# A message-passing layer on one core: 8-bit bins and places, nine message buffers for six, and two sets of loads issued at other times

## The chip, the core and the metric

The kernel runs on one core of one Trainium2 chip. Its time is the device time of one launch in microseconds; of several launches the median is given. The five engines are named as in the profile: PE multiplies matrices (PEld is its weight load), DVE and ACT work on vectors, POOL is GpSimd, and SP does nothing here but issue DMAs in the order in which they stand in the program. ACT and POOL issue DMAs too.

## The reference, cut to what matters

12500 nodes with 128 features each, 400000 edges sorted by destination, 20 attributes for each edge. The code calls the sorted side `dst` and the random side `src`; messages are *gathered* at `dst` and *summed* at `src`.

```python
h = max(layernorm(x), 0) @ W_in2f.T                      # 12500 x 128
Wij = smu(f_ij @ W_f1.T + b_f1) @ W_f2.T + b_f2          # 400000 x 128, from the 20 attributes
x_ij = h[dst] * Wij * edge_weight[:, None]               # one message for each edge
agg = segment_sum(x_ij, src)                             # 12500 x 128
out = x + smu(agg @ W_o1.T + b_o1) @ W_o2.T + b_o2
```

## The kernel before, in words

**Tiles, groups, supers.** 128 edges are a tile, 4 tiles a group (`GRP`), 2 groups a super (`SUP` = 8 tiles). There are 3125 tiles, 782 groups and 391 supers. The main loop runs over the groups in the order `seq`; its counter is `p`, and the group at `p` is `g`.

**What a group costs.** PE makes the hidden layer (`hide`), ACT bends it (`bend`), PE weighs it (`weigh`, tile `pw`) and gathers the node rows with a one-hot matrix (`gather`, tile `ph`), ACT copies them (`take`, tile `hg`), DVE multiplies the two into the message tile `ms` (`mix`, L997, or L986 and L987 for a paired group). A row of `ms` is 128 features and, as a 129th number, the edge's place within its bin of 128 source nodes.

**Sorting through DRAM.** The sum over `src` is a sort into 98 bins. `bins` and `count` find for each edge the next free row of its bin (DVE marks the bins and keeps running counts, PE counts in tile `pc`, DVE reads it out in L774 and writes row numbers `ix` in L796). POOL then scatters each tile of `ms` to those rows of a DRAM store `buf` with an indirect DMA (`scatter_rows`, L1067): four scatters a group. To have fewer, every third group is paired: two of its tiles are merged into the other two rows' slots (`permute`, `take_pairs`), it takes two scatters, and what did not fit goes out as tile `lt` with a later group, its host, which has five. There are 2933 scatters in all. POOL's scatters stand in no order written by hand, but they follow the groups; PE, DVE, ACT and SP run in the order of the program text.

**Buffers that tie the engines to POOL.** `ms` has six buffers, `ix` eight, `lt` three. An engine that writes one of them waits until the scatter that read it last has landed.

**Epochs and passes.** The supers are cut into ten epochs (`PARTS`). While epoch k is scattered into one store, the store of epoch k-1 is summed in a *pass*: SP fetches chunks of it (`fetch`, L1098, tile `rw`, four buffers), DVE turns the places into a one-hot matrix (`choose`, L1112, tile `se`), PE multiplies (`add`, L1125) and the sums go to `agg`. For epochs 1 to 7 a pass starts with group 7 of the epoch (`LANDED`, called `i` in `chores`): `begin` fetches four chunks, `choose` makes the first one-hot matrix in group 8 and `add` starts in group 9, where it also asks for the second matrix. Each finished chunk fetches the one four ahead. The last two epochs' groups are computed early among the others; their messages are kept in DRAM (`kept_rows`, written by a DMA that ACT issues, L1037) and come back at the end, where only scatters and the last passes are left.

**Chunks of the edge list.** `dst` and `src` come in seven chunks of 512 tiles (`head_of`). For each, `fetched` loads both (SP, L405 and L406, 256 KB each), `based` reads the first destination of each group (DVE, L409), `binned` computes the bins of 128 (`hi_f`, 16-bit float) and `placed` the places (`lo_b`, bfloat16). A timetable of `due` entries says in which slot each stage runs; there are three slots a group. `known`, slot 106, is where the rows of x have all been read.

Of the kernel before, what the change touches and what calls it, by code (L numbers as in the profile page):

```python
# [20 lines left out]
P = 128  # L21
# [8 lines left out]
SUP = 8  # L30
# [20 lines left out]
def gnn_kernel(  # L51
# [294 lines left out]
    with tc.tile_pool(name="ld", bufs=4) as ld, \  # L346
            tc.tile_pool(name="edge", bufs=2) as edge, \
            tc.tile_pool(name="cnt", bufs=3) as cnt, \
            tc.tile_pool(name="msg", bufs=6) as msg, \
            tc.tile_pool(name="row", bufs=4) as rowp, \  # L350
            tc.tile_pool(name="ps1", bufs=1, space=PSUM) as ps1, \
            tc.manual_schedule(engines={ET.PE, ET.DVE, ET.Activation, ET.SP}):
# [36 lines left out]
        def head_of(c, bank=bank):  # L389


            a, n = c * CH, min(CH, NT - c * CH)
            s0, m = a // GRP, (n + GRP - 1) // GRP
            rw = rowp.tile([P, ROWS, ROW], F32, name="rw").rearrange("p q r -> p (q r)")
            di, si, rel = rw[:, 0:n].bitcast(I32), rw[:, CH:CH + n].bitcast(I32), rw[:, 2 * CH:2 * CH + n]
            sf = rw[:, 0:n]
            spare_rows = parts_tile().rearrange("p n k d -> p (n k d)")
            rb = spare_rows.bitcast(U8)[:, :GRP * P].rearrange("p (n e) -> p n e", e=P)
            z = 0 if c else FEW
            base_f = spare_rows.bitcast(F32)[0:1, P:P + CH // GRP]  # L400
            cells = [(j * P, min(P, n - j * P)) for j in range((n + P - 1) // P)]
            kept = [None]

            def fetched():
                nc.sync.dma_start(di, dst_col[:, a:a + n])  # L405
                nc.sync.dma_start(si, src_col[:, a:a + n])  # L406

            def based():
                nc.vector.tensor_copy(base_i[:, s0:s0 + m], di[0:1, 0:n:GRP])  # L409
                nc.vector.tensor_copy(base_f[:, :m], base_i[:, s0:s0 + m])  # L410
                if c == 0:
                    nc.vector.memset(base_f[:, :FEW // GRP], 0.0)
                nc.vector.tensor_copy(rel, di)

            def spread():
                pb = kept[0] = bank("pb")
                flat = pb.rearrange("p j e -> p (j e)")[:, :m * GRP].rearrange("p (s t) -> p s t", t=GRP)
                nc.tensor.matmul(flat, onesb[0:1], base_f[:, :m].unsqueeze(2).to_broadcast([1, m, GRP]),
                                 start=True, stop=True)

            def lowered():
                nc.vector.tensor_sub(rel, rel, kept[0].rearrange("p j e -> p (j e)")[:, :n])

            def turned():
                pd = kept[0] = bank("pd")
                for j, (o, w) in enumerate(cells):
                    nc.tensor.transpose(pd[:w, j, :], rel[:, o:o + w], ident)

            def written():
                w = cells[-1][1]  # L430
                whole = len(cells) - (w < P)
                if whole:
                    nc.scalar.activation(rb[:, :whole], kept[0][:, :whole], AF.Copy)
                    nc.sync.dma_start(rel_dram[0, a * P:(a + whole * P) * P].rearrange("(c t e) -> t c e", t=P, e=P),
                                      rb[:, :whole])
                if w < P:
                    nc.scalar.activation(rb[:w, whole], kept[0][:w, whole], AF.Copy)
                    nc.sync.dma_start(rel_dram[0, (a + whole * P) * P:(a + n) * P].rearrange("(t e) -> t e", e=P),
                                      rb[:w, whole])

            def limits():
                nc.vector.tensor_reduce(lh[:, 0, c:c + 1], rel, op=ALU.min, axis=AX.X)
                nc.vector.tensor_reduce(lh[:, 1, c:c + 1], rel, op=ALU.max, axis=AX.X)

            def bounded():
                most = edge.tile([1, 1], F32, name="most")
                nc.vector.tensor_reduce(most, base_f[:, :early], op=ALU.max, axis=AX.X)
                nc.vector.tensor_scalar(bad[0:1, 2:3], most, float(HEAD * P - WIN), None, op0=ALU.is_gt)
                nc.vector.tensor_scalar(base_i[:, :early], base_f[:, :early], float(HEAD * P - WIN), None, op0=ALU.min)

            def binned():
                whole_bins(hi_f[:, a + z:a + n], sf[:, z:], si[:, z:])

            def placed():
                nc.vector.scalar_tensor_tensor(lo_b[:, a + z:a + n], hi_f[:, a + z:a + n], -float(P), sf[:, z:],
                                               op0=ALU.mult, op1=ALU.add)
# [190 lines left out]
        def mark_bins(s):  # L647
# [8 lines left out]
            m = n // 2  # L656
            nc.vector.tensor_tensor(es[:, :m], eo[:, 0:2 * m:2], eo[:, 1:2 * m:2], op=ALU.add)
            marked[s] = (eo, es)

        def places_of_counts(g, n):  # L660

# [5 lines left out]
        def bins(g):  # L667
# [7 lines left out]
            if g in first:  # L675
                k = first[g]
                m = FEW if g == 0 else tiles_of(k)
                if s_of(g) < EARLY:
                    begins[k] = (t, cnt.tile([P, max(n for _, n in eps_of) * SUP], F32, name="hic", bufs=2))
                else:  # L680
                    begins[k] = (t, cnt.tile([P, eps_of[k][1] * SUP], F32, name=f"hic{k}", bufs=1))
                nc.vector.tensor_scalar(begins[k][1][:, :m], hi_f[:, t:t + m], float(CAP[k]), -BIG, op0=ALU.mult, op1=ALU.add)
# [94 lines left out]
        def number(g):  # L777
# [338 lines left out]
        def add(k, b, q):  # L1116
# [11 lines left out]
                return  # L1128
            if i == SPAN[k] - 1 or b == NB - 1:
                rows_in.pop(c), sel.pop(c)  # L1130
                fetch(k, behind(k, c, AHEAD))
            if g == GRP - 1 or b == NB - 1:
                dst = agg[:, (b - g) * P:(b + 1) * P]
# [54 lines left out]
        LEFT = 24  # L1188

        def few_places():  # L1190
            nc.vector.scalar_tensor_tensor(lo_b[:, 0:FEW], hi_f[:, 0:FEW], -float(P), ssf, op0=ALU.mult, op1=ALU.add)

        def other_starts():
            m = tiles_of(0)
            nc.vector.tensor_scalar(begins[0][1][:, FEW:m], hi_f[:, FEW:m], float(CAP[0]), -BIG, op0=ALU.mult, op1=ALU.add)

        def spread_tiles(g, pb, a, n):

# [86 lines left out]
        rounded(hi_f[:, 0:FEW], ssf, ss.bitcast(F32))  # L1285
        for s in range(2):
            double(s, nc.vector)
        bins(0)
# [127 lines left out]
        for i, (b, n) in enumerate(of_rows):  # L1416
# [37 lines left out]
        def chores(g):  # L1454
# [29 lines left out]
            if i == begins_at:  # L1484
# [224 lines left out]
        def homes():  # L1709
# [7 lines left out]
            yield ones_tile().bitcast(F32)  # L1717
            for name in ("hg", "sm", "hg", "sm", "sm"):
                yield edge.tile([P, GRP * P], F32, name=name, bufs=3 if name == "sm" else 2)
            yield zero[:, 0:GRP * P]  # L1720

        places = homes()
        rows_got = []
# [64 lines left out]
        def place_of_left(g):  # L1788
# [4 lines left out]
            ix = ranks[g] = cnt.tile([P, GRP + 1], I32, name="ix", bufs=8)  # L1793
# [258 lines left out]
```

## Time and profile before

| | |
|---|---|
| median of 3 runs | 3901.89 us (3888.05 to 3905.70) |
| the profiled execution | 3893.4 us, of which the span of the profile is 3891.4 us |
| mean granted TensorE clock | 0.950 |
| busy, share of the span | PE 84%, PEld 73%, DVE 79%, ACT 73%, POOL 74% |
| DMA | 904.80 MB, 233 GB/s |
| first and last scatter start | 12.69 us, 3831.15 us |

In a row of the timeline the first number is the start in us from the begin of the span, the second the length in us, and what stands in brackets is how long the engine had been idle and what ended that. In a row of waits stand the total in us, the number of times and the longest. POOL's busy share counts the 0.96 us of a scatter and not the 0.30 us between two of them.

### The profile page before, as it was taken

Reading aid. Unit: us, or ns where it says so; the run is one execution under the profiler, and the core shown is the slowest. Engines: PE = TensorE matmul, PEld = TensorE weight load, DVE = VectorE, ACT = ScalarE, POOL = GpSimd, SP = SyncE. Lnnn points to the kernel's source line nnn. Section 1 sums busy time; section 2 is a strip of 40 time slices with the busy share of each in tenths; the row PEclk is TensorE's granted clock in tenths of the full one; section 3 lists DMA queues with packets and bytes.
Section 4 is the critical chain, followed back from the end, with each engine's and each line's share of the span. In section 5 each row is a group of like instructions: output and inputs, shape, how many; then the busy total and the mean of one; then the engine's idle time right before and its main releaser. Section 6 shows DMA issues by size and latency. Waiting matters only on the chain. (4 is left out here: it accounts for less than half of the span.)

```text
span 3891.4 us, 89320 instructions
## 1 busy us (share of the span) xinstructions
PE 3269.7 (84%) x27191; PEld 2852.2 (73%) x27505; DVE 3066.1 (79%) x8171; ACT 2829.8 (73%) x8043; POOL 2895.7 (74%) x2977
## 2 busy tenths in 40 slices
PE   7666767888888888888888889898899888988767
PEld 3245555777777877777777778888788788888657
DVE  6877776778777888878888878888888788887557
ACT  7766666878788888888888888887778777776102
POOL 6767777777677777777777777777777777777776
PEclk9978898999999999999999999999999999999889
DMA  5887878889898777787877878888888878887988
GB/s 166 221 218 225 233 220 243 242 244 255 244 266 233 227 216 229 222 236 221 231 223 217 236 212 247 233 229 233 232 232 250 238 223 235 240 237 204 282 268 240
DMA packets 663934, 904.80 MB, mean 233 GB/s; under 512 B 180371, under 2 KB 463127, under 8 KB 663321
## 3 DMA queue, kind: packets, MB, share of 16 engines
q1 hardware_dynamic: 556025, 666.99, 62.9%
q0 software_dynamic: 100112, 219.73, 17.5%
q10 hardware_dynamic: 7312, 12.29, 0.9%
q8 instruction: 223, 3.65, 0.4%
q14 instruction: 262, 2.15, 0.2%
HBM read 500.66 MB, written 398.03 MB: 231 GB/s over the span
## 5 line engine op out<-in xcount | busy, mean ns | idle before, releaser
L1067 POOL DMA_INDIRECT buf<-ms,ix x2578 | 2510.5, 974 | 861.7 <-issue 583.5
L1125 PE MATMUL pg<-se,rw 128*128 128x128 f32 x8036 | 1173.3, 285 | 97.3 <-DVE agg L1138 37.8
L1125 PEld LDWEIGHTS pg<-se,rw 128*128 128x128 f32 x8036 | 1043.3, 195 | 151.8 <-DVE agg L1138 54.3
L940 ACT ACTIVATE hg<-ph,w_sb 128x128 f32<-128x128 f32 x2784 | 786.1, 363 | 481.9 <-PE ph L921 467.6
L965 PE MATMUL pw<-w_f,ge 128*128 128x128 f32 x5568 | 784.3, 286 | 40.0 <-DVE ms L997 14.7
L965 PEld LDWEIGHTS pw<-w_f,ge 128*128 128x128 f32 x5568 | 705.1, 199 | 60.6 <-ACT ms L1045 16.0
L1112 DVE TENSOR_TENSOR se<-irow_ps,rw 128x1536 f32<-128x1536 f32 (+1 forms) x345 | 587.3, 1702 | 73.9 <-DMA rw<-buf 54.5
L774 DVE TENSOR_REDUCE pc<-pc 128x4 f32<-128x392 f32 (+1 forms) x782 | 463.5, 593 | 150.3 <-PE pc L730 142.4
L616 ACT ACTIVATE oh<-rbc,nrow 128x512 bf16<-128x512 uint8 x724 | 538.6, 744 | 22.5 <-DMA rbc<-rel_dram 22.5
L617 ACT ACTIVATE oh<-oh,onesb 128x512 bf16<-128x512 bf16 x742 | 535.3, 721 | 24.2
L997 DVE TENSOR_TENSOR ms<-pw,hg 128x512 f32<-128x512 f32 x513 | 351.4, 685 | 181.8 <-DMA buf<-ms,ix 63.7
L730 PE MATMUL pc<-eo,tri 128*128 128x392 f16 x782 | 265.1, 339 | 134.9 <-DVE ix L796 91.1
L854 PE MATMUL pt<-cd,mt 128*128 128x129 f32 (+1 forms) x2304 | 309.5, 286 | 81.4 <-DVE at L834 69.4
L854 PEld LDWEIGHTS pt<-cd,mt 128*128 128x128 f32 x2304 | 284.9, 199 | 95.8 <-issue 52.5
L921 PE MATMUL ph<-hw,oh 126*128 126x128 bf16 x2784 | 280.7, 225 | 25.6 <-ACT hg L940 19.5
L893 ACT ACTIVATE ge<-pu 128x512 f32<-128x512 f32 x452 | 275.0, 608 | 18.3 <-PE pu L885 17.1
L730 PE MATMUL pc<-so,ones_h 128*128 128x392 f16 (+1 forms) x965 | 279.2, 312 | 0.4 <-DVE so L696 0.4
L967 PE MATMUL pw<-wls,f 128*128 128x128 bf16 x2784 | 275.8, 223 | 0.0
L730 PEld LDWEIGHTS <-ones_h 128*128 128x128 f16 x1554 | 153.6, 99 | 143.1 <-issue 25.0
L921 PEld LDWEIGHTS <-oh 126*128 126x128 bf16 x2784 | 219.6, 100 | 46.4 <-issue 25.0
L653 DVE TENSOR_TENSOR eo<-irow_ps,ed 128x784 f16<-128x784 f16 x391 | 218.0, 558 | 22.5 <-ACT ed L643 19.6
L1067 POOL DMA_INDIRECT buf<-lt,ix x192 | 186.6, 972 | 59.9 <-issue 27.8
(337 smaller groups left out, 4959.8 us busy)
## 6 DMA issues: line engine op xcount, KB each, us to landing
rw<-buf SPq DMA_DIRECT2D x292, 774.0 KB
f<-f_parts SPq DMA_DIRECT2D x370, 240.0 KB
buf<-zero SPq DMA_DIRECT2D x146, 387.0 KB
rbc<-rel_dram SPq DMA_DIRECT2D x389, 128.0 KB
buf<-ms,ix POOLq DMA_INDIRECT x2578
f_parts<-hs SPq DMA_DIRECT2D x104, 360.0 KB
rw<-buf SPq DMA_DIRECT2D x49, 645.0 KB
f_parts<-hs SPq DMA_DIRECT2D x106, 240.0 KB
```

The lines of the kernel that those rows point to most:

```text
L616: nc.scalar.activation(oh, loaded[s][1][:, o:o + n], AF.Abs, bias=pneg if s < FEW // SUP else nrow)
L617: nc.scalar.activation(oh, oh, AF.Relu, scale=-1.0, bias=onesb[:, 0:1])
L730: nc.tensor.matmul(to, by, of, start=start, stop=stop, skip_group_check=True)
L774: nc.vector.tensor_reduce(sl[:, :n], pc[:, :n], op=ALU.max, axis=AX.X)
L854: nc.tensor.matmul(po[:, j * (ROW + 1):j * (ROW + 1) + w], pp[:, o:o + P], cd[:, i, :w], start=(i == 0), stop=(i == 1))
L921: nc.tensor.matmul(ph[:, j * P:(j + 1) * P], oh[:3 * WIN, a:a + P], hw[:3 * WIN, g % PER, :], start=True, stop=True)
L940: nc.scalar.activation(hg[:, j * P:(j + 1) * P], rows_of[g][:, j * P:(j + 1) * P], AF.Copy, scale=w_sb[:, t + j:t + j + 1])
L965: nc.tensor.matmul(pw[:, a:a + P], ge[:, a:a + P], w_f2, start=(a == 0), stop=False, skip_group_check=True)
L997: nc.vector.tensor_tensor(ms[:, :n, 0:P], pw.rearrange("p (j f) -> p j f", f=P)[:, :n], hg.rearrange("p (j f) -> p j f", f=P)[:, :n], op=A ...
L1067: i = nc.gpsimd.indirect_dma_start(out=(wide if g in host or g in pair_no else bufs)[k][:, :], out_offset=bass.IndirectOffsetOnAxis(ap=ix, ...
L1112: nc.vector.tensor_tensor(se[:, a:a + n], own.unsqueeze(1).to_broadcast([P, n, P]), rows_in[c][:, a:a + n, P:P + 1].to_broadcast([P, n, P] ...
L1125: nc.tensor.matmul(pgs[0][:, g, :], rows_in[c][:, o, 0:P], sel[c][:, o, :], start=(q == 0), stop=(q == Q[k] - 1))
```

## The change

- **8-bit values.** `hi_f` (float16) and `lo_b` (bfloat16) become `hi_b` and `lo_b` in unsigned 8 bit. Bins are below 98 and places below 128. Every reader and writer stays where it was; only the type differs. The room goes to the next point, and the x rows that were read at the end into these two tiles get other homes.
- **Nine `ms` buffers for six**, and twelve `ix` buffers for eight. `lt` keeps its three.
- **Destinations of early chunks sooner.** For chunks whose time lies before `known` (1, 2 and 3) `fetched` is due `SOONER` = 9 slots, three groups, earlier. The tile that `based` and `written` need is taken when `based` runs.
- **First fetches of a pass one per group.** `begin` fetches one chunk, and `ask` one more in each of the next three groups, for the passes of epochs 1 to 7. The others still fetch four at once.

```diff
-    hi_w = const.tile([P, NT + NT % 2], F16, name="hi_w")
-    hi_f = hi_w[:, 0:NT]
-    lo_w = const.tile([P, NT + NT % 2], BF, name="lo_b")
-    lo_b = lo_w[:, 0:NT]
+    hi_w, lo_w = [const.tile([P, -(-NT // 4) * 4], U8, name=name) for name in ("hi_b", "lo_b")]
+    hi_b, lo_b = hi_w[:, 0:NT], lo_w[:, 0:NT]
...
-            tc.tile_pool(name="msg", bufs=6) as msg, \
+            tc.tile_pool(name="msg", bufs=9) as msg, \
...
             def binned():
-                whole_bins(hi_f[:, a + z:a + n], sf[:, z:], si[:, z:])
+                whole_bins(hi_b[:, a + z:a + n], sf[:, z:], si[:, z:])
...
-            of = hi_f[:, t:t + n].unsqueeze(2).to_broadcast([P, n, 2])
+            of = hi_b[:, t:t + n].unsqueeze(2).to_broadcast([P, n, 2])
...
-                ix = cnt.tile([P, GRP + 1], I32, name="ix", bufs=8)
+                ix = cnt.tile([P, GRP + 1], I32, name="ix", bufs=12)
...
-        def begin(k):
-            for c in order_of[k][:AHEAD]:
+        def begin(k, at_once):
+            asked.clear()
+            ask(k, at_once)
+
+        asked = []
+
+        def ask(k, n):
+            for c in order_of[k][len(asked):min(AHEAD, len(asked) + n)]:
                 fetch(k, c)
+                asked.append(c)
...
+        SOONER = 9
         for c in range(1, NC):
...
             t = 5 + (c - 1) * apart_heads
-            for i, f in enumerate(stages):
+            due(t + 0.5 - (SOONER if t < known else 0), stages.pop(0))
+            t = math.floor(t) + 3
+            for i, f in enumerate(stages, 1):
...
-                begin(k - 1)
+                begin(k - 1, 1 if begins_at == LANDED else AHEAD)
+            elif i > begins_at and summing == k - 1:
+                ask(k - 1, 1)
```

PE, DVE, ACT and POOL keep their instructions in the same order; only SP's order changes. On SP, the loads of chunk 2 stood before as follows (`zero` clears a store, `f_parts` and `f` are edge attributes, `agg` takes rows of x, `rbc` takes destinations as 8-bit offsets, `hw` node rows):

```order
L223 DMA buf_63<-zero 128x2x387 x2
L1595 DMA f_parts<-se 120x3x512
L1595 DMA f_parts<-se 120x2x512
L1595 DMA f_parts<-se 120x512
L1382 DMA agg<-in_x 128x12x128
L223 DMA buf_63<-zero 128x2x387
L405 DMA rw<-in_dst_col 128x512
L406 DMA rw<-in_src_col 128x512
L576 DMA f_142<-in_f_t 20x1024
```

The same two loads, on SP, after the change (the code's lines have other numbers):

```order
L602 DMA hw<-h_head 126x1x128
L222 DMA buf_63<-zero 128x2x387 x2
L402 DMA rw<-in_dst_col 128x512
L403 DMA rw<-in_src_col 128x512
L577 DMA f_141<-in_f_t 20x1024
L587 DMA rbc<-rel_dram 128x1024
```

They have moved ahead of the loads of one super (`f_141`, `rbc`, two `hw`), three clears, three writes of `f_parts` and one read of x.

The second place on SP is the start of the second pass, in epoch 2, which fetches from `buf_64`. Before:

```order
L1098 DMA rw<-buf_64 128x2x774 x4
L570 DMA f_140<-f_parts 120x1024
L586 DMA rbc<-rel_dram 128x1024
L600 TENSOR_LOAD base_i
L600 ISA x2
L601 ISA
L601 DMA hw<-h_dram 126x1x128
```

After, on SP, where the same super's loads now stand between the first fetch and the second:

```order
L1103 DMA rw<-buf_64 128x2x774
L571 DMA f_140<-f_parts 120x1024
L587 DMA rbc<-rel_dram 128x1024
L601 TENSOR_LOAD base_i
L601 ISA x2
L602 ISA
L602 DMA hw<-h_dram 126x1x128
L601 TENSOR_LOAD base_i
L601 ISA x2
L602 ISA
L602 DMA hw<-h_dram 126x1x128
L1103 DMA rw<-buf_64 128x2x774
```

Three of the four fetches have moved behind loads that they stood ahead of: the second behind one super's, the third behind three `f_parts` writes more, the fourth behind two further supers.

More of the change, by code (lines that the diff above doesn't have):

```diff
@@ L181, in gnn_kernel @@
     kept_rows = dram.tile([P, NT - kept_tile, ROW], F32, name="kept_rows")
-    hi_w = const.tile([P, NT + NT % 2], F16, name="hi_w")
-    hi_f = hi_w[:, 0:NT]
-    lo_w = const.tile([P, NT + NT % 2], BF, name="lo_b")
-    lo_b = lo_w[:, 0:NT]
+    assert NB <= 256
+    hi_w, lo_w = [const.tile([P, -(-NT // 4) * 4], U8, name=name) for name in ("hi_b", "lo_b")]
+    hi_b, lo_b = hi_w[:, 0:NT], lo_w[:, 0:NT]
     w_sb = const.tile([P, NT], F32, name="w_sb")
@@ L396, in head_of @@
             sf = rw[:, 0:n]
-            spare_rows = parts_tile().rearrange("p n k d -> p (n k d)")
-            rb = spare_rows.bitcast(U8)[:, :GRP * P].rearrange("p (n e) -> p n e", e=P)
             z = 0 if c else FEW
-            base_f = spare_rows.bitcast(F32)[0:1, P:P + CH // GRP]
+            rb = base_f = None
             cells = [(j * P, min(P, n - j * P)) for j in range((n + P - 1) // P)]
@@ L408, in based @@
             def based():
+                nonlocal rb, base_f
+                spare_rows = parts_tile().rearrange("p n k d -> p (n k d)")
+                rb = spare_rows.bitcast(U8)[:, :GRP * P].rearrange("p (n e) -> p n e", e=P)
+                base_f = spare_rows.bitcast(F32)[0:1, P:P + CH // GRP]
                 nc.vector.tensor_copy(base_i[:, s0:s0 + m], di[0:1, 0:n:GRP])
@@ L451, in binned @@
             def binned():
-                whole_bins(hi_f[:, a + z:a + n], sf[:, z:], si[:, z:])
+                whole_bins(hi_b[:, a + z:a + n], sf[:, z:], si[:, z:])
             def placed():
-                nc.vector.scalar_tensor_tensor(lo_b[:, a + z:a + n], hi_f[:, a + z:a + n], -float(P), sf[:, z:],
+                nc.vector.scalar_tensor_tensor(lo_b[:, a + z:a + n], hi_b[:, a + z:a + n], -float(P), sf[:, z:],
                                                op0=ALU.mult, op1=ALU.add)
@@ L658, in mark_bins, with starts_tile @@
             marked[s] = (eo, es)
+        def starts_tile():
+            assert max(n for _, n in eps_of) * SUP <= GRP * P
+            return cnt.tile([P, GRP * P], F32, name="hic", bufs=2)
         def places_of_counts(g, n):
@@ L678, in bins @@
                 if s_of(g) < EARLY:
-                    begins[k] = (t, cnt.tile([P, max(n for _, n in eps_of) * SUP], F32, name="hic", bufs=2))
+                    begins[k] = (t, starts_tile())
                 else:
                     begins[k] = (t, cnt.tile([P, eps_of[k][1] * SUP], F32, name=f"hic{k}", bufs=1))
-                nc.vector.tensor_scalar(begins[k][1][:, :m], hi_f[:, t:t + m], float(CAP[k]), -BIG, op0=ALU.mult, op1=ALU.add)
+                nc.vector.tensor_scalar(begins[k][1][:, :m], hi_b[:, t:t + m], float(CAP[k]), -BIG, op0=ALU.mult, op1=ALU.add)
             k = epoch[s]
@@ L1130, in add @@
                 rows_in.pop(c), sel.pop(c)
+                assert len(asked) == min(AHEAD, len(order_of[k]))
                 fetch(k, behind(k, c, AHEAD))
@@ L1190, in few_places @@
         def few_places():
-            nc.vector.scalar_tensor_tensor(lo_b[:, 0:FEW], hi_f[:, 0:FEW], -float(P), ssf, op0=ALU.mult, op1=ALU.add)
+            nc.vector.scalar_tensor_tensor(lo_b[:, 0:FEW], hi_b[:, 0:FEW], -float(P), ssf, op0=ALU.mult, op1=ALU.add)
         def other_starts():
             m = tiles_of(0)
-            nc.vector.tensor_scalar(begins[0][1][:, FEW:m], hi_f[:, FEW:m], float(CAP[0]), -BIG, op0=ALU.mult, op1=ALU.add)
+            nc.vector.tensor_scalar(begins[0][1][:, FEW:m], hi_b[:, FEW:m], float(CAP[0]), -BIG, op0=ALU.mult, op1=ALU.add)
         def spread_tiles(g, pb, a, n):
@@ L1284, in gnn_kernel @@
         nc.scalar.activation(spare[:, 1:2], eps, AF.Gelu)
-        rounded(hi_f[:, 0:FEW], ssf, ss.bitcast(F32))
+        rounded(hi_b[:, 0:FEW], ssf, ss.bitcast(F32))
         for s in range(2):
@@ L1716, in homes @@
                 yield parts_tile().rearrange("p n k d -> p (n k d)").bitcast(F32)[:, :GRP * P]
-            yield ones_tile().bitcast(F32)
+            for _ in range(2):
+                yield ones_tile().bitcast(F32)
+            for _ in range(2):
+                yield starts_tile()
             for name in ("hg", "sm", "hg", "sm", "sm"):
@@ L1720, in homes @@
             yield zero[:, 0:GRP * P]
+            yield edge.tile([P, 6 * P], F32, name="mt", bufs=2)[:, :GRP * P]
         places = homes()
@@ L1792, in place_of_left @@
             nc.vector.tensor_reduce(sl[:, 0:1], pc[:, 0], op=ALU.max, axis=AX.X)
-            ix = ranks[g] = cnt.tile([P, GRP + 1], I32, name="ix", bufs=8)
+            ix = ranks[g] = cnt.tile([P, GRP + 1], I32, name="ix", bufs=12)
             nc.vector.scalar_tensor_tensor(ix[:, 0:1], sl[:, 0:1], BIG + CAP[k] - 1, left_of[g][1],
```

## The prediction

> **What bounds the kernel now.** I read the busy shares first, then POOL's own timeline, then its scatters by stage, then the waits of the engines that feed it.
>
> ```profile
> span 3891.4 us, 89320 instructions
> PE 3269.7 (84%) x27191; PEld 2852.2 (73%) x27505; DVE 3066.1 (79%) x8171; ACT 2829.8 (73%) x8043; POOL 2895.7 (74%) x2977
> ```
>
> By shares PE and DVE lead and POOL is among the last. The timeline of POOL in the middle of the run says otherwise:
>
> ```profile
> 1501.39 0.96 POOL L1067 DMA_INDIRECT buf<-ms,ix  x1 [0.30 <-issue]
> 1502.65 0.96 POOL L1067 DMA_INDIRECT buf<-ms,ix  x1 [0.30 <-issue]
> ```
>
> A scatter counts as 0.96 us of work, but the next starts 1.26 us after it (1.262 over longer runs of them) and the 0.30 us between have no releaser: 1.262 us is the period of a POOL that is never short of work. The windows of the scatter line give, by stage, POOL's busy time in scatters and in brackets their number; then come PE's granted clock, the DMA engines' busy share and GB/s:
>
> ```profile
> 0.00:300.00 300.00, 202.26 (x208) 0.90 0.75 202
> 300.00:800.00 500.00, 380.94 (x387) 0.89 0.82 234
> 800.00:1130.00 330.00, 235.43 (x243) 0.96 0.88 249
> 1130.00:1700.00 570.00, 429.55 (x442) 0.98 0.80 230
> 1700.00:2200.00 500.00, 378.95 (x390) 0.97 0.80 226
> 2200.00:2700.00 500.00, 367.80 (x380) 0.98 0.81 229
> 2700.00:3340.00 640.00, 486.04 (x501) 0.97 0.84 236
> 3340.00:3832.00 492.00, 374.01 (x387) 0.93 0.84 248
> ```
>
> Length less count times 1.262 is what POOL lost: 37.5 us up to 300 (12.69 of them before the first scatter), then 11.6, 23.3, 12.2, 7.8, 20.4, 7.7 and 3.6. So of 3832 us up to the end of the last scatter 3708 are 2938 counted periods (a few scatters are counted on both sides of a border); the 59 us behind it are the tail. From 300 to 3340 the six losses add up to 83 us. Part is no starvation: 429.55/442 = 0.972 us a scatter is 0.014 above the usual 0.958, over 2343 scatters 33 us of long ones. That leaves 50 us between 300 and 3340, and some 22 before, that a better fed POOL could win.
>
> The Trainium skill ("Perfetto Trace Analysis", Identifying the Most-Contended Engine) says to take the engine with the highest occupancy, and that PE's occupancy is no good measure; of the others here that is DVE at 79%. By that rule more buffers towards POOL win nothing. The trace contradicts it: in the stage from 1130 to 1700 the 442 periods fill 558 of 570 us.
>
> **Destinations sooner.** Where POOL starves early, its gaps are these:
>
> ```profile
> 178.94 1.13 POOL L1067 DMA_INDIRECT buf<-ms,ix  x1 [5.62 <-ACT ms L1035]
> 207.67 0.95 POOL L1067 DMA_INDIRECT buf<-ms,ix  x1 [2.97 <-ACT ms L1035]
> 213.55 0.96 POOL L1067 DMA_INDIRECT buf<-ms,ix  x1 [1.14 <-ACT ms L1035]
> 269.35 0.96 POOL L1067 DMA_INDIRECT buf<-ms,ix  x1 [5.42 <-issue]
> ```
>
> The first and the last stand just behind two stalls of DVE, which wait for the loads that move. SP issued those loads 8.0 and 6.8 us before DVE went on:
>
> ```profile
> 172.34 0.26 DVE L409 COPY base_i<-rw 1x128 int32<-1x128 int32 x1 [12.09 <-DMA rw<-in_dst_col]
> 264.52 0.26 DVE L409 COPY base_i<-rw 1x128 int32<-1x128 int32 x1 [7.42 <-DMA rw<-in_dst_col]
> ```
>
> ```profile
> 150.49 1.29 SPq L576 DMA_DIRECT2D f<-in_f_t  x1
> 164.35 1.04 SPq L405 DMA_DIRECT2D rw<-in_dst_col  x1
> 243.29 1.70 SPq L223 DMA_DIRECT2D buf<-zero  x3
> 257.73 0.53 SPq L405 DMA_DIRECT2D rw<-in_dst_col  x1
> ```
>
> Chunk 2's load now stands ahead of the `f` of 150.49, 13.9 us sooner, and lands at about 158.4; DVE came to it at 160.25. Chunk 3's stands before the third of the clears at 243.29, about 13 us sooner, lands near 251, and DVE came at 257.1. Both waits go. POOL wins its gaps less the 0.30: 5.32 and 5.12. The rest of the 12.09 us becomes lead, and covers the 2.67 and 0.84 that follow. Sum 13.9 us. Chunk 1 had a short wait with POOL hardly touched: 0. Bounds: 0, if the landing slips by as much as the issue gains, and 19.5, both waits in full; I take 13.9, since DVE's slack of 2 and 6 us is above the spread of the two landings, 1.2 us. What is moved past: each pair of 256 KB loads delays the super's loads, clears and writes behind it by two issues, 2 us by the rows above; those loads serve groups five or six later, some 25 us, so nothing is late. The waits for chunks 4 to 6 stay; they lie between 300 and 800, where POOL lost 11.6 us in all, 5.4 of them (387 x 0.014) by long scatters.
>
> **Nine buffers.** The engines ahead of POOL were held by full buffers in two stretches, 300 to 800 and 1700 to 2000, by the rows of waits in these windows (first three rows, then three):
>
> ```profile
> ACT ms L1047 <- DMA buf<-ms,ix: 11.3, 6, 3.2
> DVE ms L997 <- DMA buf<-ms,ix: 10.9, 5, 3.6
> DVE ms L987 <- DMA buf<-ms,ix: 4.6, 5, 1.9
> ...
> DVE ms L997 <- DMA buf<-ms,ix: 11.4, 9, 4.0
> ACT ms L1047 <- DMA buf<-ms,ix: 4.2, 2, 3.0
> DVE ms L987 <- DMA buf<-ms,ix: 4.2, 1, 4.2
> ```
>
> Each is followed by one in which POOL starves: 800 to 1700 (losses 23.3 + 12.2, less 685 x 0.014 = 9.6, so 26 us) and 2200 to 2700 (20.4 less 5.3, so 15 us). A lead won while held is kept until a stall eats it. Three buffers more are three groups, at 2933/782 = 3.75 scatters each about 11 scatters, 14 us of lead. The ring of three `lt` tiles, unchanged, allows less. Here is a host's `lt` in the later, well fed part, and the write that reuses its buffer:
>
> ```profile
> 2876.13 0.96 POOL L1067 DMA_INDIRECT buf<-lt,ix  x1 [0.30 <-DVE se L1112]
> ```
>
> ```profile
> 2888.78 0.32 ACT L866 ACTIVATE lt<-pt 128x130 f32<-128x130 f32 x1
> ```
>
> From 2877.09 to 2888.78 are 11.7 us; a scatter takes about 4 to land, as the longest held waits above say, so some 7.7 us of lead fit before ACT is held there instead. Between 7.7 and 14 I take 11 us for each stretch, 22 in all. Bounds: 0, if the `lt` ring holds at once, and the whole 50.
>
> Not all is to be had: two gaps of one stall, 3.8 and 7.7 us beyond the 0.30, come when POOL's lead was long gone, and ACT there has no buffer to wait for but a DMA of its own to issue (the like of the second row, 6.5 us idle behind the first):
>
> ```profile
> 991.13 0.95 POOL L1067 DMA_INDIRECT buf<-ms,ix  x1 [4.12 <-ACT ms L1047]
> 1003.88 0.95 POOL L1067 DMA_INDIRECT buf<-ms,ix  x1 [8.02 <-ACT hg L940]
> ```
>
> ```profile
> 803.86 1.12 ACT L1035 ACTIVATE ms<-pt,w_sb 128x128 f32<-128x128 f32 x4
> 811.47 0.33 ACTq L1037 DMA_DIRECT2D kept_rows<-ms  x1
> ```
>
> That stays; what is late next is this issue, and behind it PE.
>
> **8-bit values.** No row of before reads a bin as 8 bit. The nearest are ACT's two passes over a one-hot matrix, one from 8 bit and one from bfloat16:
>
> ```profile
> L616 ACT ACTIVATE oh<-rbc,nrow 128x512 bf16<-128x512 uint8 x724 | 538.6, 744 | 22.5 <-DMA rbc<-rel_dram 22.5
> L617 ACT ACTIVATE oh<-oh,onesb 128x512 bf16<-128x512 bf16 x742 | 535.3, 721 | 24.2
> ```
>
> 23 ns more over 512 elements, so for the 2 to 16 elements of the readers here below 1 ns each; over about 1300 readers the ends are -1 and +1 us by size, +30 if the 23 ns were fixed. All of it is on ACT, off POOL's path: 0.
>
> **First fetches apart.** In the second pass the four were issued together, and the one-hot matrices of the first two chunks were made without a wait:
>
> ```profile
> 1231.10 7.41 SPq L1098 DMA_DIRECT2D rw<-buf  x4
> 1240.48 2.94 SPq L601 DMA_DIRECT2D hw<-h_dram  x2
> ```
>
> ```profile
> 1242.38 1.75 DVE L1112 TENSOR_TENSOR se<-irow_ps,rw 128x1536 f32<-128x1536 f32 x1
> 1247.20 1.75 DVE L1112 TENSOR_TENSOR se<-irow_ps,rw 128x1536 f32<-128x1536 f32 x1
> ```
>
> Now the second fetch stands behind one super's loads, 5 us by these rows (1238.51 to 1243.42). With the 8.0 us that a 256 KB load took, and 2.2 more for 774 KB at 233 GB/s, it lands 15 us behind the first; it is needed 16.1 us behind it. So 0 us, with a wait of a few us possible in each of seven passes, covered by the lead; a gain of 0 too, as no gap of POOL stands behind 1231. With a longer lead the first fetch can itself have to wait for the last scatter of the epoch, while loads queue behind it on SP; but then POOL has that lead to work off. In the last stage POOL lost 3.6 us, its long scatters alone explain that, and the tail waits for the last scatter: 0.
>
> **Sum.** 13.9 + 22 = 36 us off 3893.4, so 3857. The three runs' median is 8.5 above that execution, which lies within their spread of 17.6; I add half, 4, and predict 3861.
>
> **Rivals.**
> *DVE or PE is the bound after all.* Then the buffers win 0: only the early stalls count, 14 us, 3883 with the 4 added, no change within the measurement. For it: POOL loses most from 800 to 1130, behind the held stretch and not in it, so the engines ahead are no faster than POOL there. Against: the held stretches themselves. The Trainium skill's rule above would have it so.
> *The `lt` ring is no limit and the lead lasts*: 14 + 50 = 64, 3833.
> *Slower: the second fetch of a pass.* Its place is `choose` of chunk 2, seven times. If it lands x us late, DVE stops for x, and POOL starves for x less its lead of about 10 us (two groups). To end 20 us behind, the 36 won included, 56 us must be lost, 8 in each pass, which gives 3917: it decides when the fetch lands 18 us late, 34 us behind the first. Against: the 7 to 8 us in which the loads of chunks 2 and 3 landed.
> *The loads come no sooner*, since SP or the DMA rings are behind by then: the 14 fall away, 3875.
>
> **How the numbers follow.** 0.5%, 20 us, is what a measurement of this kernel can tell from no change. Chances: forecast, both terms (a gain of 20 to 50) 0.60; longer lead (50 to 64) 0.09; DVE or PE the bound 0.18; loads no sooner 0.06, of which half is still faster; slower 0.07. Faster 0.72, same 0.21, slower 0.07. The range leaves out the slower rival and the ends: from 3830, the longer lead less half of the 8.5 us to the median, to 3893, where 4 us of the early stalls are won and nothing else.
>
> **What would show it.** Right: no wait for `in_dst_col` of over 2 us at chunks 2 and 3, three left behind; early gaps of POOL gone, so 212 to 220 scatters up to 300; in the stages from 800 to 1700 and 2200 to 2700 some 8 scatters more each; `ms` waits down, and ACT held at `lt` (0.3 us in all before). Wrong: POOL's period above 1.262, long waits of `se` on `rw` at the starts of passes, or the losses by stage unchanged while `ms` waits are gone, which would mean that the feeders bind.

## The result, and the profile after

The changed kernel takes 3879.0 us (median of 14 runs, 3866.5 to 3886.9), the kernel before 3895.8 us on the same chip (14 runs, 3888.1 to 3905.7). The ratio is 0.9955, with a 95% interval of 0.9944 to 0.9965: 17 us faster, where 36 were forecast. The chips used below differ a little (the kernel before took 3895.8, 3886.6 and 3877.8 us), so only ratios from one chip are compared. One set of four ran on a chip where the kernel before took 5990 us; it is told of by itself.

The head of the page of after, to set beside that of before:

```profile
span 3875.5 us, 89505 instructions
PE 3289.4 (85%) x27505; PEld 2851.7 (74%) x27505; DVE 3066.3 (79%) x8171; ACT 2831.6 (73%) x8043; POOL 2889.8 (75%) x2977
```

The shares say nothing about where the 17 us came from. The windows of the scatter line do (columns as before: POOL busy in scatters, their number, PE's clock, DMA share, GB/s):

```profile
0.00:300.00 300.00, 208.74 (x215) 0.90 0.77 207
300.00:800.00 500.00, 376.47 (x384) 0.88 0.83 234
800.00:1130.00 330.00, 235.68 (x243) 0.95 0.88 251
1130.00:1700.00 570.00, 424.79 (x438) 0.97 0.80 227
1700.00:2200.00 500.00, 378.74 (x393) 0.98 0.81 229
2200.00:2700.00 500.00, 375.22 (x387) 0.99 0.82 233
2700.00:3340.00 640.00, 487.15 (x502) 0.96 0.85 236
```

Length less count times 1.262 gives the losses: 28.7, 15.4, 23.3, 17.2, 4.0, 11.6, 6.5, where before had 37.5, 11.6, 23.3, 12.2, 7.8, 20.4, 7.7. So 9 us came from the first stage and 13 from 1700 to 2700. From 300 to 1700, 9 us were given back. The start of the n-th scatter in the two traces, counted from 0, shows the same as one line (one execution of each; executions of the changed kernel differ by up to 20 us):

| scatter | 50 | 350 | 400 | 900 | 950 | 1300 | 1550 | 2050 | 2932 |
|---|---|---|---|---|---|---|---|---|---|
| after less before, us | +0.6 | -9.7 | -5.3 | -4.1 | -1.8 | +0.1 | -0.8 | -12.3 | -15.4 |

The tail behind the last scatter is 58.8 us; it was 59.3.

**What the early loads won, and what came late instead.** In after, the waits of DVE for chunks 2 and 3 are gone; a read of x and chunks 4 to 6 are left (timeline of DVE, then of POOL):

```profile
151.36 0.29 DVE L235 BATCH_NORM_STATS2 st<-agg 128x6 f32<-128x128 f32 x1 [3.96 <-DMA agg<-in_x]
331.23 0.26 DVE L410 COPY base_i<-rw 1x128 int32<-1x128 int32 x1 [10.93 <-DMA rw<-in_dst_col]
410.11 0.26 DVE L410 COPY base_i<-rw 1x128 int32<-1x128 int32 x1 [11.89 <-DMA rw<-in_dst_col]
494.20 0.16 DVE L410 COPY base_i<-rw 1x14 int32<-1x14 int32 x1 [15.04 <-DMA rw<-in_dst_col]
```

```profile
499.54 0.95 POOL L1072 DMA_INDIRECT buf<-lt,ix  x1 [6.85 <-DVE ix L804]
```

Before, the wait for chunk 6 was 13.7 us, and POOL's gap behind it this:

```profile
523.49 0.96 POOL L1067 DMA_INDIRECT buf<-lt,ix  x1 [1.37 <-DVE ix L799]
```

It is 6.85 us now, because POOL had moved 9 to 10 us forward by then and DVE only 4.7 to 5: the same stall met a lead that was 5 us shorter. DVE had been 12.7 us forward at the place of the old wait for chunk 3 (the same instruction in both traces), and 2.4 at 320. Between the two, the engines ahead of POOL wait for the loads of their supers, which SP issues only 0.2 to 4.2 us sooner than before. These are rows of waits from 140 to 330, before and then after:

```profile
ACT oh L616 <- DMA rbc<-rel_dram: 0.6, 1, 0.6
```

```profile
ACT oh L617 <- DMA rbc<-rel_dram: 9.7, 4, 3.5
```

**The buffers.** The rows of waits of the whole run, after:

```profile
DVE ms L1002 <- DMA buf<-ms,ix: 21.1, 21, 2.5
ACT lt L871 <- DMA buf<-lt,ix: 17.7, 11, 5.6
ACT ms L1052 <- DMA buf<-ms,ix: 10.3, 6, 6.2
ACT ms L1050 <- DMA buf<-ms,ix: 5.9, 7, 1.6
```

The waits of DVE and ACT at `ms` add up to 39 us, where they were 160. The six of the row at L1052 each stand behind the issue of a write to `kept_rows`: they belong to the stall told of below, and no buffer is short there. All of the 17.7 us at `lt` lie between 2700 and 3340, where POOL lacks nothing. The first held stretch did win a lead, and lost it again at the first pass. By the same instructions in both traces, DVE was 4.7 us forward at what was 600 before, 13.8 at 660, 6.5 at 665 and 3.8 at 675. Between the last three stand these rows of DVE, and on SP the fetches that they wait for:

```profile
657.93 1.76 DVE L1117 TENSOR_TENSOR se<-irow_ps,rw 128x1536 f32<-128x1536 f32 x1 [6.25 <-DMA rw<-buf]
...
667.30 1.76 DVE L1117 TENSOR_TENSOR se<-irow_ps,rw 128x1536 f32<-128x1536 f32 x1 [3.26 <-DMA rw<-buf]
```

```profile
649.63 0.41 SPq L222 DMA_DIRECT2D buf<-zero  x1
650.17 0.38 SPq L1103 DMA_DIRECT2D rw<-buf  x1
650.59 0.86 SPq L1595 DMA_DIRECT2D sm<-in_f_t  x1
651.50 0.50 SPq L571 DMA_DIRECT2D f<-f_parts  x1
652.11 0.43 SPq L587 DMA_DIRECT2D rbc<-rel_dram  x1
653.62 2.92 SPq L602 DMA_DIRECT2D hw<-h_dram  x2
656.60 0.63 SPq L222 DMA_DIRECT2D buf<-zero  x1
657.27 3.51 SPq L1103 DMA_DIRECT2D rw<-buf  x2
```

SP issues row after row there. Its waits between 600 and 660 are short; the longest row and that for the scatters of the epoch are:

```profile
SPq L602 <- PE pc L735: 1.0, 2, 0.7
...
SPq L1103 <- DMA buf<-ms,ix: 0.4, 1, 0.4
```

The first fetch lands 7.8 us after its issue, and DVE, now early, is there before it. The second costs 3.26 us more. That is the lead that should have covered the stalls from 800 on.

**What stalls there.** ACT ends a message tile at 982.23 and issues its write to `kept_rows` at 985.47; what it waited for is given as a clear of another store, a DMA of SP. The printed rows leave out the wait instructions, but the trace has them. The DMAs of SP and ACT signal their landing on eight semaphores, 352 DMAs on each, and in front of this issue stands a wait for semaphore 110, which the write is to use and which the clear issued at 977.24 used last. So it is the program that makes ACT wait until a DMA has landed with whose data it has nothing to do. POOL starves behind it:

```profile
981.11 1.12 ACT L1040 ACTIVATE ms<-pt,w_sb 128x128 f32<-128x128 f32 x4
985.47 0.33 ACTq L1042 DMA_DIRECT2D kept_rows<-ms  x1
985.91 0.21 ACT L1052 ACTIVATE ms<-lo_b 128x4 f32<-128x4 uint8 x1 [3.68 <-DMA buf<-zero]
```

```profile
999.09 0.96 POOL L1072 DMA_INDIRECT buf<-ms,ix  x1 [7.95 <-ACT hg L945]
```

Over the 46 such writes ACT stood 28.9 us before its issue; before the change it was 28.7. Before 14 of them it stood for over 0.1 us, and at all 14 there is such a wait for the write's own semaphore.

### The profile page after: what moved, and what is told of

Its sections match the earlier page's. It is cut to its first block, busy times and chain, and to the rows that moved or that the text cites. A ratio compares the mean times of both kernels' runs of the same rounds, so it can differ in the third digit from the quotient of the medians.

```text
span 3875.5 us, 89505 instructions
## 1 busy us (share of the span) xinstructions
PE 3289.4 (85%) x27505; PEld 2851.7 (74%) x27505; DVE 3066.3 (79%) x8171; ACT 2831.6 (73%) x8043; POOL 2889.8 (75%) x2977
## 4 chain that ended last, share of the span: by engine, by line
PE 31%; DVE 17%; DMA 17%; issue 8%; ACT 8%; POOL 7%; SPq 1%; DVEq 0%; ACTq 0%; POOLq 0%
DMA buf<-ms,ix 11%; PE pg L1130 10%; POOL buf L1072 7%; PE pw L970 6%; PE pt L859 5%; PE pc L735 3%; ACT hg L945 3%; DVE se L1117 3%; DVE pc L779 2%; DMA rbc<-rel_dram 2%; DVE mt L822 2%; DVE ms L1002 2%; PE ph L926 2%; DVE eo L654 2%; DMA buf<-lt,ix 2%
## 5 line engine op out<-in xcount | busy, mean ns | idle before, releaser
L970 PE MATMUL pw<-w_f,ge 128*128 128x128 f32 x5568 | 778.3, 284 | 12.7 <-DVE ms L1002 7.6
L1072 POOL DMA_INDIRECT buf<-lt,ix x192 | 185.9, 968 | 65.5 <-issue 28.7
```

The costliest lines, as they stand in the source:

```text
L970: nc.tensor.matmul(pw[:, a:a + P], ge[:, a:a + P], w_f2, start=(a == 0), stop=False, skip_group_check=True)
L1072: i = nc.gpsimd.indirect_dma_start(out=(wide if g in host or g in pair_no else bufs)[k][:, :], out_offset=bass.IndirectOffsetOnAxis(ap=ix, ...
```

## The experiments

**The parts alone.** Four kernels on one chip (before: 3886.6 us, 27 runs), each the changed kernel with parts taken back. The 8-bit values stay in all. The edit of `ix`, shown once below, stands in two places of the code; dots mark what is left out between two places.

Buffers only:

```diff
-            due(t + 0.5 - (SOONER if t < known else 0), stages.pop(0))
+            due(math.floor(t) + 0.5, stages.pop(0))
...
-                begin(k - 1, 1 if begins_at == LANDED else AHEAD)
+                begin(k - 1, AHEAD)
```

> The changed kernel with the destination loads and the first fetches of a pass back in their old places: what is left is the 8-bit values, nine ms and twelve ix buffers. Theory A (a lead won in a held stretch lasts only until a pass starts: its first one-hot matrix waits for a fetch that itself waits for the epoch's last scatter, so DVE gives the lead back): the first held stretch, 300 to 800, wins 0, as the first pass starts at 654 inside it; the second, 1700 to 2000, wins the 11 us that stand between scatters 1550 and 2050 of the traces of before and after; 10 to 13 us off in all, ratio 0.9967 to 0.9974. Theory B (the prediction as it stood: two stretches of 11): 22 us off, 0.9944. Theory C (DVE and PE bind, buffers win nothing): 0, ratio 1.000.

Measured: 3877.6 us, ratio 0.9976 (0.9966 to 0.9986), 9 us off. Nearest to theory A, a little below it; that the second stretch wins 11 is not borne out (see the buffers in the next section). The wait at the first pass stands here too, with the fetches together, so it is the first fetch and not the spreading that takes most of that lead:

```profile
657.42 1.76 DVE L1117 TENSOR_TENSOR se<-irow_ps,rw 128x1536 f32<-128x1536 f32 x1 [6.37 <-DMA rw<-buf]
```

One part of theory A is wrong: in the changed kernel the first fetch did not wait for the epoch's last scatter (the 0.4 us above); it stood in SP's own row of issues.

Early destinations only:

```diff
-            tc.tile_pool(name="msg", bufs=9) as msg, \
+            tc.tile_pool(name="msg", bufs=6) as msg, \
...
-                ix = cnt.tile([P, GRP + 1], I32, name="ix", bufs=12)
+                ix = cnt.tile([P, GRP + 1], I32, name="ix", bufs=8)
...
-                begin(k - 1, 1 if begins_at == LANDED else AHEAD)
+                begin(k - 1, AHEAD)
```

> The changed kernel with six ms and eight ix buffers and the first fetches of a pass all at once: what is left is the earlier load of the destinations of chunks 1 to 3, beside the 8-bit values. Theory A (POOL wins 9 to 10 us by 300, but DVE is only 5 us ahead by 320, so the lead in front of the wait for chunk 6 is 5 us shorter and that wait costs POOL 5 to 6 us which it cost before nearly nothing): 4 to 6 us off, ratio 0.9985 to 0.9990, with a gap of POOL of 5 to 7 us near 500. Theory B (the prediction as it stood): 14 us off, 0.9964, and no new gap. Theory C (the stall's time is lost anyway in the stages from 800 on): 0.

Measured: 3877.8 us, 0.9978 (0.9969 to 0.9987), 9 us off: between A and B. The price at chunk 6 is there, but smaller than A had it:

```profile
496.94 0.95 POOL L1072 DMA_INDIRECT buf<-lt,ix  x1 [3.07 <-DVE ix L804]
```

In five traces with early loads of chunks 1 to 3 alone, from the changed kernel and those below, the gap was 6.85, 3.07, 8.32, 1.33 and under 1.3 us. Two of these are the changed kernel itself, on two chips (6.85 and 1.33), so that the price of this stall is not a fixed one.

First fetches apart only:

```diff
-            due(t + 0.5 - (SOONER if t < known else 0), stages.pop(0))
+            due(math.floor(t) + 0.5, stages.pop(0))
...
-            tc.tile_pool(name="msg", bufs=9) as msg, \
+            tc.tile_pool(name="msg", bufs=6) as msg, \
...
-                ix = cnt.tile([P, GRP + 1], I32, name="ix", bufs=12)
+                ix = cnt.tile([P, GRP + 1], I32, name="ix", bufs=8)
```

> The changed kernel with the destination loads in their old places, six ms and eight ix buffers: what is left is the first fetches of a pass one per group, beside the 8-bit values. Theory A and the prediction (with the shorter lead of six buffers DVE comes to the second matrix after its fetch has landed): 0, ratio 0.999 to 1.001, no wait of se for rw over 1 us at the starts of the first five passes. Theory B (the second fetch lands late at each pass start by some us): 3 to 10 us slower, 1.001 to 1.0025. Theory C (supers' loads come sooner at each pass start): 3 to 10 us faster, 0.9975 to 0.999.

Measured: 3883.8 us, 1.000 (0.9991 to 1.001). Theory A. One wait of `se` for `rw`, 2.31 us at the first pass, went over A's 1 us; POOL had the lead for it. With the 8-bit values in it as well, this puts both together at nothing, within 4 us. The three parts add up: 9 + 9 + 0 = 18, against 17 for the whole.

Without the spreading:

```diff
-                begin(k - 1, 1 if begins_at == LANDED else AHEAD)
+                begin(k - 1, AHEAD)
```

> The changed kernel with the first four fetches of a pass issued together, as before; early destinations and nine buffers stay. Theory A (issuing them apart costs lead: in the first pass the second fetch, issued 7 us behind the first, made DVE wait 3.3 us): 2 to 4 us faster than the changed kernel, ratio to before 0.9945 to 0.9950, and the wait of se for rw at 667 gone, while the one at 658 (6.3 us, for the first fetch) stays. Theory B (prediction: worth 0): equal to the changed kernel, 0.9955. Theory C (issuing apart is what keeps the supers' loads from standing behind 3.1 MB, 13 us at 233 GB/s): 4 to 13 us slower than the changed kernel, 0.9965 to 0.9988.

Measured: 3865.0 us, 0.9939 (0.9926 to 0.9953). The wait at 667 is gone, the one at 657 stays (6.24 us), as A has it. But the interval overlaps that of the changed kernel on the other chip, so that the gain of some 5 us is likely and not shown; C is out.

**The stalls themselves.** Four kernels on another chip (before: 3877.8 us, 11 runs), the changed kernel among them.

> The changed kernel once more, on the same chip as the next three, as their base. Ratio to before as measured, 0.9955 (0.9944 to 0.9965); a theory by which the gain hangs on the chip, and not on the program, would have it outside this interval.

Measured: 3856.0 us, 0.9951 (0.9937 to 0.9965). The gain stands on this chip too.

All six early:

```diff
-            due(t + 0.5 - (SOONER if t < known else 0), stages.pop(0))
+            due(t + 0.5 - SOONER, stages.pop(0))
```

> The changed kernel with the destination loads of chunks 4 to 6 nine slots sooner too. In the changed kernel DVE waits for them 10.9, 11.9 and 15.0 us, and POOL starves 6.6 us behind the last. Theory A (what POOL wins before the first pass stays won, what DVE wins beyond it is given back at the first pass, whose first fetch waits for the epoch's last scatter): the three waits and the gap near 500 go, 5 to 8 us faster than the changed kernel. Theory B (the groups from 800 to 1300 run at the feeders' own pace, and what POOL won before is lost there): 0 to 2 us. Theory C (all of DVE's 38 us becomes lead and covers the stalls up to 1000 too): 20 us or more.

Measured: 3852.0 us, 0.9939 (0.9924 to 0.9954), 4 us below the changed kernel and within the spread. The three waits of DVE, 38 us in the changed kernel, are gone, and so is the gap near 500, which was only 1.33 us on this chip; C is out, A and B are not told apart. The 38 us went into other waits. Rows of waits from 300 to 660, of the changed kernel on this chip and then of this one:

```profile
ACT oh L617 <- DMA rbc<-rel_dram: 18.4, 7, 4.7
DVE oh L615 <- DMA rbc<-rel_dram: 1.5, 1, 1.5
```

```profile
ACT oh L617 <- DMA rbc<-rel_dram: 46.8, 16, 6.5
DVE oh L615 <- DMA rbc<-rel_dram: 14.3, 8, 3.3
```

DVE is 20.8 us in front of the changed kernel at 484, 6.0 at 600 and no longer at 800. What it and ACT wait for are loads of the supers that SP issues, and SP itself waits for only 38 of these 360 us and otherwise works through its own row. So SP's row cuts the lead well before the first pass. No run shortened that row, so this limit is read from the traces and not tested. The first pass adds its waits, as in the changed kernel:

```profile
641.59 1.76 DVE L1117 TENSOR_TENSOR se<-irow_ps,rw 128x1536 f32<-128x1536 f32 x1 [5.84 <-DMA rw<-buf]
```

The writes of `kept_rows` from SP:

```diff
-                nc.scalar.dma_start(kept_rows[:, t - kept_tile:t - kept_tile + n, :], ms[:, :n, :])
+                nc.sync.dma_start(kept_rows[:, t - kept_tile:t - kept_tile + n, :], ms[:, :n, :])
```

> The changed kernel with the 46 writes of kept_rows issued by SP instead of ACT. Theory A (the gaps of POOL at 807 to 837, 986 and 999, 1085 and 1092 come from ACT standing at that DMA): these gaps, 6.4, 10.5 and 3.1 us beyond the normal 0.30, go, and the kernel is 10 to 20 us faster than the changed one. Theory B (SP then waits for ACT's message tile and everything behind it on SP, the loads of later supers, comes late): gaps move to waits for rbc and f, 0 to 30 us slower. Theory C (the gaps come from PE's work for these groups, not from the issue): the gaps stay within 2 us each, 0.

Measured: 3835.8 us, 0.9895 (0.9878 to 0.9913): 20 us below the changed kernel, with intervals that don't touch, and 42 below before. Theory A, at its upper end. The window of the scatter line from 800 to 1130, first of the changed kernel on this chip and then with this edit, and SP's waits at these writes:

```profile
800.00:1130.00 330.00, 244.49 (x253) 0.98 0.90 258
```

```profile
800.00:1130.00 330.00, 251.03 (x260) 0.98 0.91 260
```

```profile
SPq L1042 <- ACT ms L1050: 34.0, 6, 9.0
SPq L1042 <- ACT ms L1040: 18.7, 7, 9.8
SPq L1042 <- ACT ms L1052: 9.1, 4, 4.7
```

260 scatters stand where there were 253 (243 before the change, on the first chip): the loss of that stage is down to 1.9 us. Behind the first 36 us only one gap of POOL is over 1 us longer than the usual 0.30 (3.24 at 2612.82). SP now waits 62 us in the place of ACT, and POOL does not starve for it, so the loads behind these writes still come in time.

All three edits:

```diff
-            due(t + 0.5 - (SOONER if t < known else 0), stages.pop(0))
+            due(t + 0.5 - SOONER, stages.pop(0))
...
-                begin(k - 1, 1 if begins_at == LANDED else AHEAD)
+                begin(k - 1, AHEAD)
...
-                nc.scalar.dma_start(kept_rows[:, t - kept_tile:t - kept_tile + n, :], ms[:, :n, :])
+                nc.sync.dma_start(kept_rows[:, t - kept_tile:t - kept_tile + n, :], ms[:, :n, :])
```

> The changed kernel with three edits: destination loads of all six chunks sooner, the first fetches of a pass issued together, and the writes of kept_rows issued by SP. Theory A (each removes a stall of its own): the sum of the two runs before it and of 4 to 6 us for the fetches, 15 to 30 us faster than the changed kernel. Theory B (they feed one lead, which the start of each pass cuts back): no more than the best of them alone.

Measured: 3835.0 us, 0.989 (0.9873 to 0.9908). Theory B: no more than the best alone. Once POOL doesn't starve behind 36 us, a longer lead has nothing to cover. The changed kernel with the edit of `kept_rows` alone is as fast, and simpler. Whether the kernel before with that edit alone would be as fast too is open: it was only measured on the chip that comes next.

**A chip on which something else binds.** The last four ran where the kernel before takes 5990 us (35 runs, 5953 to 6486). They were to settle what the spreading costs, whether the buffers are still needed beside that edit, and the `lt` ring.

The changed kernel again, without an edit:

> The changed kernel once more, as the base of the next three on their chip: 0.9950 to 0.9955 of before.

The fetches together, the same edit as above:

> The changed kernel with the first four fetches of a pass issued together, beside the changed kernel on one chip. Theory A (issuing them apart costs lead, 3 us at the first pass): 3 to 7 us faster than the changed kernel. Theory B (what it costs at the first pass is cut off there anyway, since the first fetch sets how far ahead DVE may be): 0 to 2 us apart.

The kernel before, with the edit of `kept_rows`:

```diff
-                nc.scalar.dma_start(kept_rows[:, t - kept_tile:t - kept_tile + n, :], ms[:, :n, :])
+                nc.sync.dma_start(kept_rows[:, t - kept_tile:t - kept_tile + n, :], ms[:, :n, :])
```

> The kernel before with one edit: SP issues the 46 writes of kept_rows. Six ms buffers, late destinations, fetches together. Theory A (in the middle stages the nine buffers win only what stalls at this DMA take; without the stalls six are enough): the stalls of the middle stages go, 20 to 26 us faster than before, 0.9933 to 0.9949, and the changed kernel with the same edit, 0.9895, keeps only its early 10 to 15 us above it. Theory B (six buffers cannot bridge the other stalls, so buffers and edit add up): 12 to 18 us faster, 0.9954 to 0.9969, with gaps of POOL over 1 us left between 1200 and 2700.

Five `lt`, eight `ms`:

```diff
-            tc.tile_pool(name="msg", bufs=9) as msg, \
+            tc.tile_pool(name="msg", bufs=8) as msg, \
...
-            lt = cnt.tile([P, ROW + 1], F32, name="lt", bufs=3)
+            lt = cnt.tile([P, ROW + 1], F32, name="lt", bufs=5)
```

> The changed kernel with five lt buffers for three and eight ms buffers for nine (no room for nine and five). Theory A (the lt ring did not limit the lead where stalls follow: in the changed kernel no wait at it stands between 300 and 2000): 0 to 3 us from the changed kernel, no wait of lt for its buffer over 1 us, and the gaps between 800 and 1700 unchanged. Theory B (the prediction: the lt ring cut each stretch from 14 to 11 us; eight ms buffers allow 9.5): 0 to 3 us slower by the lost ms buffer. Theory C (the lt ring was the limit in full): 5 to 15 us faster.

Measured, in this order: 0.9994 (0.9973 to 1.0016), 0.9985 (0.9961 to 1.0009), 0.9998 (0.9975 to 1.002), 0.996 (0.9942 to 0.9979). The last of them had 5 `lt` and 8 `ms` buffers. None of the three questions is settled by these runs, since POOL isn't the bound there. The page of the changed kernel on that chip:

```profile
PE 3878.9 (65%) x27191; PEld 3327.9 (56%) x27505; DVE 3096.2 (52%) x8171; ACT 2872.9 (48%) x8043; POOL 2887.5 (48%) x2977
PEclk8777778878877777788787888787777877888778
DMA packets 663933, 904.79 MB, mean 151 GB/s; under 512 B 180371, under 2 KB 463127, under 8 KB 663321
```

DVE, ACT and POOL are idle about half of the time, PE's granted clock is 0.795 over the run, and PE has 242 idle stretches of over 3 us, 1358 us in all, where the same kernel has 20 with 170 us on the chip of the runs just above. What makes PE stop there stays open, and so does why the last kernel won 0.4%. The one thing that these runs do show is that the change, worth 0.5% on two other chips, is worth nothing that can be measured where POOL is idle half of the time.

## Why the prediction was right, and where it was twice too large

- **The bound** was right. POOL is full at 1.262 us a scatter, and a kernel is faster by what POOL starves less: freed of one kind of stall, it went 20 us faster with DVE at 80% busy and unchanged in its work. The rule of the Trainium skill ("Perfetto Trace Analysis", Identifying the Most-Contended Engine), which points at DVE here, would have looked in the wrong place; the rival built on it, buffers worth 0, is out by 0.9976 (0.9966 to 0.9986). The time alone would not have told: 3879 lies between those of two rivals, 3883 and 3875, and further from the 3861 that was forecast.
- **Destinations sooner, 13.9 us.** The waits went as told, and 215 scatters stood up to 300, within 212 to 220. Alone the part was worth 9 us. Two steps of it failed. "Nothing is late" left out the read of x that the loads moved past, for which DVE waited 3.96 us, and the loads of the supers, which came hardly sooner than before: ACT waited 9.7 us for `rbc` up to 330. So DVE's message tiles around 350 started 4.6 us sooner, not 19.5. And the waits for chunks 4 to 6 were taken at their old price: they add up to 38 us, where they were 36, but POOL, now further forward than its feeders, paid up to 6.55 us for the last of them where it had paid 1.07.
- **Nine buffers, 22 us.** Alone they were worth 9. The first stretch won nothing that lasted. The step that failed there is "a lead won while held is kept until a stall eats it": DVE's lead was cut at the first pass, at 658 and 667, before the stalls from 800 on. The trace of before had the rows to see it: from 636 to 663 SP issues one DMA behind the other there too, so that a fetch could not follow a DVE that comes 14 us sooner. The second stretch, 1700 to 2000, looks as if it had won its 11: after less before goes from -0.8 at scatter 1550 to -12.3 at 2050. But against the same trace of before, that of the fetches alone, with six buffers, goes from -4.0 to -11.5. On that run's own chip the trace of the buffers alone is ahead of it by 0.8 us at 1550 and 4.3 at 2050. That leaves some 4 us for the buffers; how the 9 divide between the stretches is not shown.
- **The `lt` ring** was named as what limits the lead to 11 us. In the changed kernel's first trace the waits at it, 17.7 us, lie between 2700 and 3340 only, so that it limited neither stretch there. In other traces with nine buffers it did hold ACT between 1700 and 2000: 5.1 us with the buffers alone, 3.8 in the changed kernel on the other chip, 7.7 with the writes of `kept_rows` from SP. What it costs is open. The 4 us for a scatter to land were misread: a held wait begins when the engine comes, not when the scatter ends. Nine writes of `lt` that waited over 0.5 us in the first trace start 4.3 to 7.6 us behind the end of the scatter that had their buffer.
- **8-bit values and fetches apart, 0.** Right: 1.000 (0.9991 to 1.001). "A wait of a few us possible in each of seven passes" came in the first (3.26 us) and in the sixth (2.83 us at 3141, behind 1.04 for its first fetch), and at no other start of the seven over 1 us. The slower rival's place was right, its size far off the 18 us that it needed.
- **What stays late** was right: the stall at the DMA that ACT issues for `kept_rows` was named as not to be had by this change, and it is where the rest of the gain lay. What was not seen is that this one stall was worth about as much as the whole change (20 us, against 22 on the same chip), that the wait is one of the program, and that another queue can take it.

## What to carry to other kernels

Deeper buffers pay only for a lead that reaches the stall: follow the order from where the lead is won to where POOL starves, and look for what cuts it on the way, here the full row of the queue that issues the loads. Before buying lead, ask whether the stall itself can go: 46 writes issued from a queue that computes nothing were worth about as much here as three buffers, early loads and spread fetches together. Where an engine stands before a DMA of its own, look for the wait instruction in front of it and for what else uses that semaphore. And an early stall taken away moves the bound forward against its feeders, so the next stall, though no longer than it was, costs more.

## What was not expected of the hardware

- What looked like a stall of the chip is a wait in the program: ACT stood 3.24 us before a write of its own until a clear had landed that SP had issued, because the two DMAs use one semaphore. Over 46 writes it was 28.9 us. With the same writes issued by SP the kernel is 20 us faster.
- On one chip the same kernel took 1.54 times as long (5980 us to 3879), at a granted clock of 0.795 to 0.947. The clock can explain the smaller part at most: PE's busy time grew from 3289 to 3879 us, and the rest is time in which it stood still. In one run of the last kernel the recorded clock is 0.677 and the time, 5964 us, is like that of the others.
